# A two-layer graph attention kernel: where and when head 0's softmax sums of layer 1 are added, and when its accumulators are copied

## The chip, the cores and the metric

The kernel runs on one core of a Trainium2 chip. Its time is the device time of one execution in microseconds (us): a median over several runs, and one further execution that the hardware profiler recorded.

A core has five engines that run their own instruction queues in order and wait for each other through semaphores: TensorE (PE in the profile, with its weight loads as PEld), VectorE (DVE), ScalarE (ACT), GpSimd (POOL) and SyncE (SP). Transfers run on 16 DMA engines; SP and POOL issue most of them.

## What is computed

The reference, cut to what matters here. `x` is 4096 x 512, `adj` is 4096 x 4096 of zeros and ones; all is float32.

```python
# layer 0: h = relu(layernorm(x)); masked attention of 4096 x 4096 scores
x = x + L0_gnn_ref(h, adj, ...)
# layer 1: h = relu(layernorm(x)); 8 heads of 64 columns
data1 = (h @ W.T + b).reshape(4096, 8, 64)
src = jnp.einsum('nhd,xhd->nh', data1, src_proj)
trg = jnp.einsum('nhd,xhd->nh', data1, trg_proj)
e = src.T[:, :, None] + trg.T[:, None, :]      # heads x n x m
e = jnp.where(e >= 0, e, 0.01 * e)             # leaky ReLU
e = e + adj[None, :, :]
scores = jax.nn.softmax(e, axis=-1)
out = jnp.einsum('hnm,hmd->hnd', scores, data1.transpose(1, 0, 2))
x = x + out.transpose(1, 0, 2).reshape(4096, 512)
```

The change touches layer 1 alone.

## The kernel before

Layer 1 works on blocks of 1024 rows n (`WL`) and groups of four heads (`HG`): 4 x 2 = 8 groups `i`, one after the other. Inside a group it walks over 32 tiles `m` of 128 neighbours. A tile's scores lie as 128 neighbours (partitions) x 1024 rows. There are thus 256 steps, and in each step a hand-written list (`stages`) calls one function for each engine's work, some of them for tiles that lie ahead: `load` 4 tiles ahead, `exps` 1, `weigh` 1, `factors` 2, `logs` 4, `scale` 2, `gather` 0. The schedule is manual: each engine's queue has exactly the order of these calls.

What one tile costs each engine:

- SP: `load` fetches one tile of the transposed adjacency (`e`, L1066, four buffers).
- ACT: `exps` makes `ex = exp(adj)` into PSUM (L1088, one buffer). `last_exps` makes a scaled copy of it in SBUF for head 3 (`e`, L1098). `relus` makes `rl` for head 0 (L1121). In every fourth tile (`BY_LOG`: m = 3, 7, ... 31) head 0 is made on another way: `logs` (L1104) makes a ReLU, `add_logs` (L1110) adds the adjacency to it on POOL in two halves, and an exponential (L1118) gives head 0's weights directly.
- DVE: `weigh` makes the unnormalised weights `pr` of the four heads, one instruction each, in the order 3, 0, 1, 2 (`ORDER`). Heads 1 and 2 take `ex` from PSUM (L1139, `pr<-z,g_m,ex`); head 3 takes its factor from SBUF (L1139, `pr<-z,g_m,e`); head 0 takes `ex` too (L1136), and is not there in the `BY_LOG` tiles. `pr` of heads 1 to 3 has two buffers each, of head 0 three.
- PE: `gather` multiplies the weights with the values into four PSUM accumulators `pv` (L1174: 16 matmuls of 32 columns of the array, each of which shows as two instructions) and adds the softmax denominators into `dn` (L1179). Four matmuls run side by side on four groups of 32 columns.
- POOL: it adds head 3's weights into an accumulator (`acc3`, L1150; L1148 for the first two tiles). Behind it, it issues an accumulating transfer that adds head 0's weights of the tile into one of two accumulators in SBUF (L1157; plain copies for m = 0 and 1, L1155). It runs `add_logs` too: the second half for tile m + 1 ahead of the sum (and, by a wait written by hand, behind head 3's product), the first half for tile m + 2 behind it.

Head 0's sums of a tile are made either by that transfer (24 tiles, `BY_DMA`) or by PE as two extra matmuls with ones (the tiles 6, 10, 14, 18, 22, 26, 29 and 31). In the last tile PE adds the accumulators into `dn` as well.

At a group's end `gather` copies the four accumulators `pv` to SBUF on ACT (`os`, L1207). In the next group's steps `finish` then copies the denominators (`od`, L1213), inverts them, transposes the outputs two tiles at a time (`pt`, L1233), scales them (L1260), adds `x1` to them with an accumulating transfer that POOL issues (L1265), and sends them out on SP (L1263). It advances by one piece in the steps `PARTS`. After the last group `finish_last` does the same work at once.

Of the kernel before, what the change touches and what calls it, by code (L numbers as in the profile page):

```python
# [8 lines left out]
FP = mybir.dt.float32  # L9
# [6 lines left out]
P = 128  # L16
# [12 lines left out]
def kernel(  # L29
# [941 lines left out]
    nlg_m = l1.tile([P, H // HG, NT], FP, name="nlg_m")  # L971
    d0_m = l1.tile([P, H // 2, NT, 2], FP, name="d0_m")
    d0_0 = l1.tile([P, H // 2, P // 4], FP, name="d0_0")
    zo = l1.tile([P, 3], FP, name="zo")

# [19 lines left out]

    PARTS = (0, 1, 2, 4, 5, 6, 8, 9, 10, 12, 13, 14, 16, 17, 18)  # L1000
    BY_LOG = (3, 7, 11, 15, 19, 23, 27, 31)
    BY_DMA = [m for m in range(NT) if m not in (6, 10, 14, 18, 22, 26, 29, 31)]
    after = mybir.DependencyInfo(mybir.DependencyClass.Sync, mybir.DependencyReason.DATA)

    with tc.tile_pool(name="p", bufs=2) as prp, tc.tile_pool(name="s0", bufs=1) as s0, tc.tile_pool(
# [14 lines left out]
        us = {}  # L1020
        zs_, ra, ex, e3, rl, pr, acc, pv, late = {}, {}, {}, {}, {}, {}, {}, {}, {}
        ORDER = (3, 0, 1, 2)
        for t, val in ((d0_0, 0.0), (d0_m, 0.0), (zo[:, 0:2], 0.0), (zo[:, 2:3], 1.0)):
            nc.gpsimd.memset(t, val)

        def tables():
# [27 lines left out]
        row = ident.rearrange("p (r s) -> p s r", s=Q)  # L1054
        nc.vector.tensor_copy(pick, row[:, 0:2, :])
        nc.vector.tensor_tensor(pick[:, 1, 0:HV], pick[:, 1, 0:HV], row[:, 2, HV:2 * HV], ALU.add)

        def zload(i, k):
            b, g = groups[i]
# [38 lines left out]
            nc.scalar.activation(x_, ra[i, m], AF.Exp, bias=ld_m[:, h // HG, m:m + 1])  # L1098
            e3[i, m] = x_

        def logs(i, m):
            if m in BY_LOG:
                r = rlp.tile([P, WL], FP, name="lg", bufs=1)
                nc.scalar.activation(r, us[i], AF.Relu, bias=nlg_m[:, groups[i][1], m:m + 1], scale=-(1.0 - SLOPE))  # L1104
                rl[i, m] = r

        def add_logs(i, m, half, behind=None):
            if m in BY_LOG:
# [5 lines left out]
        def relus(i, m):  # L1114
            h = groups[i][1] * HG
            if m in BY_LOG:
                pr[i, m, 0] = pr0p.tile([P, WL], FP, name="pr0")
                nc.scalar.activation(pr[i, m, 0], rl.pop((i, m)), AF.Exp, bias=t_m[:, h, m:m + 1])  # L1118
                return
            r = rlp.tile([P, WL], FP, name="rl")  # L1120
            nc.scalar.activation(r, zs_[i, 0], AF.Relu, bias=ngd_m[:, h // HG, m:m + 1], scale=d_m[:, h, m:m + 1])  # L1121
            rl[i, m] = r

        def weigh(i, m, order=ORDER):
            h = groups[i][1] * HG
            x_ = ex.pop((i, m))
            for k in order:
                if (i, m, k) in pr:
                    continue
                w = (prp if k else pr0p).tile([P, WL], FP, name=f"pr{k}")  # L1130
                if k == 0 and (i, m) == (0, 0):
                    r = rlp.tile([P, WL], FP, name="rl")
                    nc.vector.tensor_scalar(r, zs_[0, 0], g_m[:, 0, 0:1], d_m[:, 0, 0:1], ALU.max, ALU.mult)
                    nc.vector.tensor_tensor(w, r, x_, ALU.mult)
                elif k == 0:
                    nc.vector.scalar_tensor_tensor(w, rl.pop((i, m)), ngd_m[:, h // HG, m:m + 1], x_,  # L1136
                                                   op0=ALU.subtract, op1=ALU.mult)
                else:
                    p_ = nc.vector.scalar_tensor_tensor(w, zs_[i, k], g_m[:, h + k, m:m + 1],  # L1139
                                                        e3.pop((i, m)) if k == 3 else x_,  # L1140
                                                        op0=ALU.max, op1=ALU.mult)
                    if k == 3:
                        add_logs(i, m + 1, 1, p_)
                pr[i, m, k] = w
            w = pr[i, m, 3]
            if m == 1:
                acc[i, 3] = acp.tile([P, WL], FP, name="acc3", bufs=1)
                nc.gpsimd.tensor_tensor(acc[i, 3], pr[i, 0, 3], w, ALU.add)  # L1148
            elif m > 1:
                nc.gpsimd.tensor_tensor(acc[i, 3], acc[i, 3], w, ALU.add)  # L1150
            add_logs(i, m + 2, 0)
            if m == 1:
                for n in range(2):
                    acc[i, 0, n] = acp.tile([P, WL], FP, name=f"acc0{n}", bufs=1)
                    nc.gpsimd.dma_start(acc[i, 0, n], pr[i, n, 0])  # L1155
            elif m > 1 and m in BY_DMA:
                nc.gpsimd.dma_start(acc[i, 0, (len(BY_DMA) + BY_DMA.index(m)) % 2], pr[i, m, 0], accum_op=ALU.add)  # L1157

        def gather(i, m):
            b, g = groups[i]  # L1160
# [2 lines left out]
                pv[i] = ([[p_v.tile([P, BL], FP, name=f"pv{c}{q}") for q in range(HV)] for c in range(2)],  # L1163
                         p_v.tile([P, BL], FP, name="dn"))
            v, dn = pv[i]
            by_pe = [u for u in range(NT) if u not in BY_DMA]
            side = sum(u < m for u in by_pe) % 2

            def values(c):
                for q in range(HV):  # L1170
                    for r in (side, 1 - side):
                        k = ((3, 0), (1, 2))[c][r]
                        for c0 in range(0, D, Q):
                            nc.tensor.matmul(v[c][q][r * D + c0:r * D + c0 + Q, :],  # L1174
                                             va[:, m, g * HG + k, c0:c0 + Q],
                                             pr[i, m, k][:, q * BL:(q + 1) * BL], start=(m == 0), stop=last)

            def den(r, w, src, q, **fl):
                nc.tensor.matmul(dn[r * Q:r * Q + w.shape[1], :], w, src[:, q * BL:(q + 1) * BL], **fl)  # L1179

            values(0 if (i, m) != (0, 0) else 1)
            if last:
                for r, a in enumerate((acc[i, 0, 0], acc[i, 3])):
                    for q in range(HV):
                        den(r * HV + q, zo[:, 1:3], a, q, start=False, stop=False)
                if m in by_pe:
                    for q in range(HV):
                        den(side * HV + q, zo[:, 1 - side:3], pr[i, m, 0], q, start=False, stop=False)
            values(1 if (i, m) != (0, 0) else 0)
            for r in (side, 1 - side):  # L1190
                for q in range(HV):
                    hk = g * 2 + r
                    den(r * HV + q, d0_m[:, hk, m, :] if m else d0_0[:, hk, :], pr[i, m, r + 1], q,
                        start=(m == 0), stop=(last and r == 1))
            if m in by_pe and not last:
                for q in range(HV):
                    den(side * HV + q, zo[:, 1 - side:3], pr[i, m, 0], q, start=False, stop=False)
            if last:
                for q in range(HV):
                    den(q, zo[:, 1:3], acc[i, 0, 1], q, start=False, stop=True)  # L1200
            for k in range(HG):
                pr.pop((i, m - 1, k), None)
            if last:
                os_ = [[osp.tile([P, BL], FP, name=f"os{c}{q}") for q in range(HV)] for c in range(2)]
                for c in range(2):
                    for q in range(HV):
                        nc.scalar.copy(os_[c][q], v[c][q])  # L1207
                late[i] = os_, dn

        def denominators(i):  # L1210
            os_, dn = late.pop(i)
            od = osp.tile([P, BL], FP, name="od")
            nc.scalar.copy(od, dn)  # L1213
            yield os_
            pd = p_t.tile([P, JT, 2, 4], FP, name="pt")
            for j in range(JT):
                nc.tensor.matmul(pd[:, j, :, :].rearrange("p e r -> p (e r)"), od[:, j * P:(j + 1) * P],  # L1217
                                 pick.rearrange("p e r -> p (e r)"), start=True, stop=True)
            yield
            rd = s0.tile([P, JT, 2, 4], FP, name="rd", bufs=2)  # L1220
            nc.vector.reciprocal(rd, pd)
            yield rd

# [18 lines left out]
        def finish(i):  # L1242
# [5 lines left out]
            next(dens)  # L1248
            yield
            rd = next(dens)  # L1250
            old = None
            for t in range(0, WT, 2):
                pt = p_t.tile([P, 2, HG, D], FP, name="pt")
                for j in range(2):
                    turn(os_, t + j, pt[:, j, :, :])
                yield
                o = iop.tile([P, 2, HG, D], FP, name="o")
                for j in range(2):
                    for r, k in enumerate(ORDER):
                        nc.scalar.activation(o[:, j, k, :], pt[:, j, r, :], AF.Copy, scale=share(rd, t + j, r))  # L1260
                    if j == 0:
                        if t:
                            nc.sync.dma_start(part(out, i, t - 2, 2), old)  # L1263
                        yield
                nc.gpsimd.dma_start(o, part(x1, i, t, 2), accum_op=ALU.add)  # L1265
                old = o
                yield
            nc.sync.dma_start(part(out, i, WT - 2, 2), old)
            yield

        def finish_last(i):

            ys = [ep.tile([P, WT // 2, HG, D], FP, name="e") for _ in range(2)]
            for n in range(2):
                nc.sync.dma_start(ys[n], part(x1, i, n * WT // 2, WT // 2))
            yield
            dens = denominators(i)
            os_ = next(dens)
            pts = []
# [65 lines left out]
        weigh(0, 0, (3, 1, 2, 0))  # L1345
        nc.vector.scalar_tensor_tensor(ngd_m, g_m[:, 0::HG, :], -1.0, d_m[:, 0::HG, :], op0=ALU.mult, op1=ALU.mult)  # L1346
        factors(0, 1)
        logs(0, 3)
        scale(0, 1)

        stages = ((load, 4), (exps, 1), (weigh, 1), (factors, 2), (logs, 4), (scale, 2), (gather, 0))
        for s in range(len(steps)):
            for f, ahead in stages:
                if s + ahead < len(steps):
# [47 lines left out]
```

## Time and profile before

| | us |
|---|---|
| median of 3 runs | 2816.33 (2816.02 to 2816.9) |
| the profiled execution: its time | 2822.91 |
| its span, first to last instruction | 2821.0 |
| layer 1's matmuls, first to last start | 1617.8 to 2809.0 |

The granted clock of TensorE was 0.993 over the span. From 2300 to 2450 us, a stretch of 150 us inside layer 1, PE is busy for 148.81 us, DVE for 147.47, ACT for 121.88 and POOL for 119.05, and the DMA engines for 0.92 of the time. The issue of a transfer is listed on POOL with a duration of its own. Tiles have no names in the profile; a tile can be told by its instructions, since only a `BY_LOG` tile has no L1136 on DVE.

In the views below, a row of the timeline is: start, duration (both us), engine, line, operation, output<-inputs, shape, count, and in brackets how long the engine had been idle before it and what ended that. A row of the waits is: who waited, for whom, total us, times, longest.

### The profile page before, as it was taken

What the parts mean: (1) busy time and instruction counts of PE and PEld (TensorE: products, weight loads), DVE (VectorE), ACT (ScalarE), POOL (GpSimd) and SP (SyncE); (2) the same over time, 40 slices, a digit from 0 to 9 for tenths busy, and PEclk for the clock granted to TensorE, in tenths of its full rate; (3) what the DMA queues carried; (4) which work ended last, traced back from release to release, by engine and by line L of the source; (5) the groups of instructions that cost most, each with busy time, mean ns of one, the idle gap of its engine ahead of it and who ended that gap; (6) DMA issues with size and microseconds to landing.
All of it is one profiled execution on the core that took longest, in us unless ns stands there. A gap on an engine that the chain in (4) does not pass through costs nothing. (4 is left out here: it accounts for less than half of the span.)

```text
span 2821.0 us, 46842 instructions
## 1 busy us (share of the span) xinstructions
PE 2758.7 (98%) x16843; PEld 1491.2 (53%) x16843; DVE 2506.5 (89%) x3424; ACT 1474.5 (52%) x2218; POOL 1396.5 (50%) x1178
## 2 busy tenths in 40 slices
PE   7999999998999999999999899999999999999998
PEld 4885444444888888888885323323222222232222
DVE  7877798898888888888886799999999999999998
ACT  2212232332124333433432188988788878888786
POOL 5323344444011010011106687887878787878786
PEclk9999999999999999999999999999999999999999
DMA  5636898887999999999977389989999998989896
GB/s 174 176 102 253 273 337 300 306 291 232 194 215 204 185 275 191 222 267 204 230 191 195 96 202 235 248 211 246 219 244 223 240 222 236 229 239 219 213 223 168
DMA packets 535992, 629.86 MB, mean 223 GB/s; under 512 B 292152, under 2 KB 346456, under 8 KB 535760
## 3 DMA queue, kind: packets, MB, share of 16 engines
q1 hardware_dynamic: 461920, 415.87, 49.5%
q0 software_dynamic: 71824, 207.07, 33.8%
q10 hardware_dynamic: 2016, 3.93, 0.4%
q8 instruction: 132, 2.16, 0.3%
q14 instruction: 100, 0.82, 0.1%
HBM read 404.23 MB, written 107.15 MB: 181 GB/s over the span
## 5 line engine op out<-in xcount | busy, mean ns | idle before, releaser
L1174 PE MATMUL pv<-pr,sup 128*32 128x512 f32 x8192 | 988.9, 594 | 8.6 <-POOL d L1344 6.2
L1150 POOL TENSOR_TENSOR acc<-acc,pr 128x1024 f32<-128x1024 f32 x240 | 577.0, 2404 | 149.3 <-DVE pr L1139 147.4
L1139 DVE SCALAR_TENSOR_TENSOR pr<-z,g_m,ex 128x1024 f32<-128x1024 f32 x512 | 630.4, 1271 | 4.1 <-ACT ex L1088 2.8
L1174 PEld LDWEIGHTS pv<-pr,sup 128*32 128x32 f32 x8192 | 283.8, 110 | 607.8 <-issue 544.9
L525 PE MATMUL pe<-he_t,he_t 128*128 128x512 f32 x896 | 389.3, 595 | 0.0
L692 ACT ACTIVATE d<-d 128x1024 f32<-128x1024 f32 x126 | 133.1, 1056 | 442.6 <-DVE d L684 230.7
L1139 DVE SCALAR_TENSOR_TENSOR pr<-z,g_m,e 128x1024 f32<-128x1024 f32 x256 | 345.3, 1349 | 3.3 <-PE pv L1174 2.8
L1088 ACT ACTIVATE ex<-e 128x1024 f32<-128x1024 f32 x256 | 263.2, 1028 | 143.2 <-DVE pr L1139 142.4
L1179 PE MATMUL dn<-pr,d_m 128*2 128x512 f32 x1984 | 319.1, 592 | 0.0
L1098 ACT ACTIVATE e<-e,ld_m 128x1024 f32<-128x1024 f32 x256 | 290.9, 1136 | 0.0
L525 PEld LDWEIGHTS pe<-he_t,he_t 128*128 128x128 f32 x896 | 170.3, 191 | 210.1 <-issue 194.8
L731 PE MATMUL po<-he_t,at 128*128 128x256 f32 x1024 | 263.8, 380 | 6.0 <-ACT he_t L742 6.0
L731 PE MATMUL po<-sup,u 128*128 128x256 f32 x1024 | 263.3, 379 | 0.0
L1136 DVE SCALAR_TENSOR_TENSOR pr<-rl,ngd_m,ex 128x1024 f32<-128x1024 f32 x191 | 242.6, 1270 | 10.3 <-ACT ex L1088 10.3
L731 PE MATMUL po<-sup,at 128*128 128x256 f32 x1024 | 243.4, 381 | 3.5 <-DVE at L702 2.3
L1121 ACT ACTIVATE rl<-z,ngd_m,d_m 128x1024 f32<-128x1024 f32 x191 | 234.8, 1229 | 1.3 <-DVE ngd_m L1346 1.3
L818 POOL DMA_DIRECT2D he_t<-he_t x56 | 48.7, 948 | 351.6 <-ACT he_t L734 299.1
L702 DVE TENSOR_TENSOR at<-d,a 128x1024 f32<-128x1024 f32 x126 | 154.1, 1223 | 71.7 <-PE po L731 34.4
L731 PEld LDWEIGHTS po<-he_t,at 128*128 128x128 f32 x1024 | 195.0, 191 | 32.9 <-issue 6.4
L731 PEld LDWEIGHTS po<-sup,at 128*128 128x128 f32 x1024 | 194.8, 191 | 32.3 <-DVE at L702 4.5
L731 PEld LDWEIGHTS po<-sup,u 128*128 128x128 f32 x1024 | 193.9, 190 | 26.0
L530 POOL DMA_DIRECT2D er_d<-mk x136 | 74.5, 548 | 239.3 <-DVE rm L527 227.2
(268 smaller groups left out, 3823.4 us busy)
## 6 DMA issues: line engine op xcount, KB each, us to landing
e<-in_adj_t_dram SPq DMA_DIRECT2D x256, 512.0 KB, 5.9
acc<-pr POOLq DMA_DIRECT2D x192, 512.0 KB, 5.9
a<-in_adj_t_dram SPq DMA_DIRECT2D x126, 512.0 KB, 5.5
ac<-in_adj_t_dram SPq DMA_DIRECT2D x124, 256.0 KB, 5.1
ar<-in_adj_dram SPq DMA_DIRECT2D x120, 256.0 KB, 4.9
ec_d<-mc POOLq DMA_DIRECT2D x120, 256.0 KB, 5.1
er_d<-mk POOLq DMA_DIRECT2D x112, 256.0 KB, 4.8
et<-er_d SPq DMA_DIRECT2D x448, 64.0 KB, 3.9
```

The costliest lines, as they stand in the source:

```text
L525: nc.tensor.matmul(pe[:, :w], he_t[i][:, k, (t % TB) * P:(t % TB + 1) * P], he_t[j][:, k, BL - w:], start=(k == 0), stop=(k == KC - 1))
L692: nc.scalar.activation(d, d, AF.Exp)
L702: nc.vector.tensor_tensor(w, d, aj.pop((n, q)), ALU.mult)
L731: nc.tensor.matmul(acc[:, j, :], A[:, j * P:(j + 1) * P], B, start=(first_ and j == 0), stop=last, skip_group_check=True)
L1088: nc.scalar.activation(x_, ra.pop((i, m)), AF.Exp)
L1098: nc.scalar.activation(x_, ra[i, m], AF.Exp, bias=ld_m[:, h // HG, m:m + 1])
L1121: nc.scalar.activation(r, zs_[i, 0], AF.Relu, bias=ngd_m[:, h // HG, m:m + 1], scale=d_m[:, h, m:m + 1])
L1136: nc.vector.scalar_tensor_tensor(w, rl.pop((i, m)), ngd_m[:, h // HG, m:m + 1], x_, op0=ALU.subtract, op1=ALU.mult)
L1139: p_ = nc.vector.scalar_tensor_tensor(w, zs_[i, k], g_m[:, h + k, m:m + 1], e3.pop((i, m)) if k == 3 else x_, op0=ALU.max, op1=ALU.mult)
L1150: nc.gpsimd.tensor_tensor(acc[i, 3], acc[i, 3], w, ALU.add)
L1174: nc.tensor.matmul(v[c][q][r * D + c0:r * D + c0 + Q, :], va[:, m, g * HG + k, c0:c0 + Q], pr[i, m, k][:, q * BL:(q + 1) * BL], start=(m = ...
L1179: nc.tensor.matmul(dn[r * Q:r * Q + w.shape[1], :], w, src[:, q * BL:(q + 1) * BL], **fl)
```

## The change

1. Head 0's sums. `BY_HALF` = (4, 8, ... 28) takes the place of the tiles that PE summed alone: of such a tile, columns 0 to 511 are summed by PE with one extra matmul (before: two), and columns 512 to 1023 by POOL into a third accumulator `acc02`, behind head 3's sum. Tile 31 stays with PE. The transfers stay 24 a group; they now also cover tiles such as 6, 10 and 29, and no longer 4, 8, ... 28. PE's four column groups are taken in an order that rotates by one with each `BY_HALF` tile.
2. The transfers' place in POOL's queue. `sums(i, m - 1)` issues tile m - 1's transfer in `weigh(m)`, behind `add_logs` of tile m + 1 and ahead of head 3's sum of tile m. The two first copies are issued one by one in the same way. The output's accumulating transfer is put on a list and issued at the same place, in a tile with m % 4 == 1; the transfer of the output to DRAM follows one piece later than before (`PARTS` gets a piece more, 22).
3. ACT's order at a group's end. Only the first accumulator is copied in `gather`. The other three and the denominators are copied in the next step (`rest`), behind that step's `exps`. The ReLU of tile 3 (`early_logs`) is made one step earlier.
4. The first tile of all now takes heads 3 and 0 ahead of 1 and 2 on PE, as all others do; `pick` gets three more small adds.

```diff
-    PARTS = (0, 1, 2, 4, 5, 6, 8, 9, 10, 12, 13, 14, 16, 17, 18)
+    PARTS = (0, 1, 2, 4, 5, 6, 8, 9, 10, 12, 13, 14, 16, 17, 18, 22)
     BY_LOG = (3, 7, 11, 15, 19, 23, 27, 31)
-    BY_DMA = [m for m in range(NT) if m not in (6, 10, 14, 18, 22, 26, 29, 31)]
+    BY_HALF = (4, 8, 12, 16, 20, 24, 28)
+    BY_DMA = [m for m in range(NT - 1) if m not in BY_HALF]
...
+        for c in range(1, 4):
+            nc.vector.tensor_tensor(pick[:, 1, 0:1], pick[:, 1, 0:1], row[:, 3, c:c + 1], ALU.add)
...
-        def logs(i, m):
-            if m in BY_LOG:
+        def logs(i, m, early=False):
+            if m in BY_LOG and early == (m == BY_LOG[0]):
...
+        due = []
+
+        def sums(i, m):
+            if m < 2:
+                acc[i, 0, m] = acp.tile([P, WL], FP, name=f"acc0{m}", bufs=1)
+                nc.gpsimd.dma_start(acc[i, 0, m], pr[i, m, 0])
+            elif m in BY_DMA:
+                nc.gpsimd.dma_start(acc[i, 0, (len(BY_DMA) + BY_DMA.index(m)) % 2], pr[i, m, 0], accum_op=ALU.add)
...
             w = pr[i, m, 3]
+            if m % 4 == 1 and due:
+                due.pop()()
+            if m:
+                sums(i, m - 1)
             if m == 1:
                 acc[i, 3] = acp.tile([P, WL], FP, name="acc3", bufs=1)
                 nc.gpsimd.tensor_tensor(acc[i, 3], pr[i, 0, 3], w, ALU.add)
             elif m > 1:
                 nc.gpsimd.tensor_tensor(acc[i, 3], acc[i, 3], w, ALU.add)
             add_logs(i, m + 2, 0)
-            if m == 1:
-                for n in range(2):
-                    acc[i, 0, n] = acp.tile([P, WL], FP, name=f"acc0{n}", bufs=1)
-                    nc.gpsimd.dma_start(acc[i, 0, n], pr[i, n, 0])
-            elif m > 1 and m in BY_DMA:
-                nc.gpsimd.dma_start(acc[i, 0, (len(BY_DMA) + BY_DMA.index(m)) % 2], pr[i, m, 0], accum_op=ALU.add)
+            if m == BY_HALF[0]:
+                acc[i, 0, 2] = acp.tile([P, BL], FP, name="acc02", bufs=1)
+                nc.gpsimd.tensor_copy(acc[i, 0, 2], pr[i, m, 0][:, BL:])
+            elif m in BY_HALF:
+                nc.gpsimd.tensor_tensor(acc[i, 0, 2], acc[i, 0, 2], pr[i, m, 0][:, BL:], ALU.add)
...
-            values(0 if (i, m) != (0, 0) else 1)
+            values(0)
             if last:
-                for r, a in enumerate((acc[i, 0, 0], acc[i, 3])):
-                    for q in range(HV):
-                        den(r * HV + q, zo[:, 1:3], a, q, start=False, stop=False)
-                if m in by_pe:
-                    for q in range(HV):
-                        den(side * HV + q, zo[:, 1 - side:3], pr[i, m, 0], q, start=False, stop=False)
+                for q in range(HV):
+                    ones(q, 1, halves(acc[i, 0, 0])[q])
+                for q in range(HV):
+                    ones(HV + q, 1, halves(acc[i, 3])[q])
+                ones(1, 1, acc[i, 0, 2])
+                for q in range(HV):
+                    ones(HV + q, 2, halves(pr[i, m, 0])[q])
+            values(1)
...
-            if m in by_pe and not last:
-                for q in range(HV):
-                    den(side * HV + q, zo[:, 1 - side:3], pr[i, m, 0], q, start=False, stop=False)
+            if m in BY_HALF:
+                ones(n, 3 if n else 1, halves(pr[i, m, 0])[0])
...
-                for c in range(2):
-                    for q in range(HV):
-                        nc.scalar.copy(os_[c][q], v[c][q])
-                late[i] = os_, dn
+                nc.scalar.copy(os_[0][0], v[0][0])
+                late[i] = os_, v, dn
+
+        def rest(i, m):
+            if i and m == 0:
+                copy_rest(i - 1)
+
+        def copy_rest(i):
+            os_, v, dn = late[i]
+            for c, q in ((0, 1), (1, 0), (1, 1)):
+                nc.scalar.copy(os_[c][q], v[c][q])
+            od = iop.tile([P, BL], FP, name="o")
+            nc.scalar.copy(od, dn)
+            late[i] = os_, od
...
+                if t > 2:
+                    nc.sync.dma_start(part(out, i, t - 4, 2), old.pop(0))
                 yield
...
-                        if t:
-                            nc.sync.dma_start(part(out, i, t - 2, 2), old)
...
-                nc.gpsimd.dma_start(o, part(x1, i, t, 2), accum_op=ALU.add)
-                old = o
+                old.append(o)
+                due.append(lambda o=o, t=t: nc.gpsimd.dma_start(o, part(x1, i, t, 2), accum_op=ALU.add))
...
-        logs(0, 3)
+        early_logs(0, 3)
...
-        stages = ((load, 4), (exps, 1), (weigh, 1), (factors, 2), (logs, 4), (scale, 2), (gather, 0))
+        stages = ((load, 4), (exps, 1), (rest, 0), (weigh, 1), (factors, 2), (logs, 4), (early_logs, 5), (scale, 2), (gather, 0))
```

More of the change, by code (lines that the diff above doesn't have):

```diff
@@ L973 @@
     d0_0 = l1.tile([P, H // 2, P // 4], FP, name="d0_0")
-    zo = l1.tile([P, 3], FP, name="zo")
+    zo = l1.tile([P, 4], FP, name="zo")
     HV = WL // BL
@@ L1022 @@
         ORDER = (3, 0, 1, 2)
-        for t, val in ((d0_0, 0.0), (d0_m, 0.0), (zo[:, 0:2], 0.0), (zo[:, 2:3], 1.0)):
+        for t, val in ((d0_0, 0.0), (d0_m, 0.0), (zo[:, 0:3], 0.0), (zo[:, 3:4], 1.0)):
             nc.gpsimd.memset(t, val)
@@ L1105, in logs, with early_logs @@
                 rl[i, m] = r
+        def early_logs(i, m):
+            logs(i, m, True)
         def add_logs(i, m, half, behind=None):
@@ L1165, in gather @@
             v, dn = pv[i]
-            by_pe = [u for u in range(NT) if u not in BY_DMA]
-            side = sum(u < m for u in by_pe) % 2
+            n = sum(u < m for u in BY_HALF) % 4
+            cols = [(n + c) % 4 for c in range(4)]
             def values(c):
                 for q in range(HV):
-                    for r in (side, 1 - side):
+                    for col in cols:
+                        r, c0 = col // 2, col % 2 * Q
                         k = ((3, 0), (1, 2))[c][r]
[L1173 to L1176, printed above, removed]
@@ L1178, in den @@
-            def den(r, w, src, q, **fl):
-                nc.tensor.matmul(dn[r * Q:r * Q + w.shape[1], :], w, src[:, q * BL:(q + 1) * BL], **fl)
-            values(0 if (i, m) != (0, 0) else 1)
-            if last:
-                for r, a in enumerate((acc[i, 0, 0], acc[i, 3])):
-                    for q in range(HV):
-                        den(r * HV + q, zo[:, 1:3], a, q, start=False, stop=False)
-                if m in by_pe:
-                    for q in range(HV):
-                        den(side * HV + q, zo[:, 1 - side:3], pr[i, m, 0], q, start=False, stop=False)
@@ L1189, in gather @@
-            values(1 if (i, m) != (0, 0) else 0)
-            for r in (side, 1 - side):
-                for q in range(HV):
-                    hk = g * 2 + r
-                    den(r * HV + q, d0_m[:, hk, m, :] if m else d0_0[:, hk, :], pr[i, m, r + 1], q,
-                        start=(m == 0), stop=(last and r == 1))
-            if m in by_pe and not last:
-                for q in range(HV):
-                    den(side * HV + q, zo[:, 1 - side:3], pr[i, m, 0], q, start=False, stop=False)
+                        nc.tensor.matmul(v[c][q][col * Q:(col + 1) * Q, :],
+                                         va[:, m, g * HG + k, c0:c0 + Q],
+                                         pr[i, m, k][:, q * BL:(q + 1) * BL], start=(m == 0), stop=last)
@@ L1198, in gather, with den, ones, halves @@
+            def den(col, w, src, **fl):
+                nc.tensor.matmul(dn[col * Q:col * Q + w.shape[1], :], w, src, **fl)
+            def ones(col, row, src, stop=False):
+                den(col, zo[:, 3 - row:4], src, start=False, stop=stop)
+            def halves(src):
+                return [src[:, q * BL:(q + 1) * BL] for q in range(HV)]
+            values(0)
             if last:
                 for q in range(HV):
-                    den(q, zo[:, 1:3], acc[i, 0, 1], q, start=False, stop=True)
+                    ones(q, 1, halves(acc[i, 0, 0])[q])
[4 more added lines that the diff above has]
+                    ones(HV + q, 2, halves(pr[i, m, 0])[q])
@@ new lines, in gather @@
+            values(1)
+            for col in cols:
+                r, q = divmod(col, HV)
+                hk = g * 2 + r
+                den(col, d0_m[:, hk, m, :] if m else d0_0[:, hk, :], halves(pr[i, m, r + 1])[q],
+                    start=(m == 0), stop=(last and r == 1))
+            if m in BY_HALF:
+                ones(n, 3 if n else 1, halves(pr[i, m, 0])[0])
+            if last:
+                for q in range(HV):
+                    ones(q, 1, halves(acc[i, 0, 1])[q], True)
@@ L1204, in gather @@
                 os_ = [[osp.tile([P, BL], FP, name=f"os{c}{q}") for q in range(HV)] for c in range(2)]
-                for c in range(2):
-                    for q in range(HV):
-                        nc.scalar.copy(os_[c][q], v[c][q])
-                late[i] = os_, dn
+                nc.scalar.copy(os_[0][0], v[0][0])
[10 more added lines that the diff above has]
+            late[i] = os_, od
         def denominators(i):
-            os_, dn = late.pop(i)
-            od = osp.tile([P, BL], FP, name="od")
-            nc.scalar.copy(od, dn)
+            os_, od = late.pop(i)
             yield os_
@@ L1219, in denominators @@
             yield
-            rd = s0.tile([P, JT, 2, 4], FP, name="rd", bufs=2)
+            rd = sp.tile([P, JT, 2, 4], FP, name="rd", bufs=2)
             nc.vector.reciprocal(rd, pd)
@@ L1250, in finish @@
             rd = next(dens)
-            old = None
+            old = []
             for t in range(0, WT, 2):
@@ L1261, in finish @@
                     if j == 0:
-                        if t:
-                            nc.sync.dma_start(part(out, i, t - 2, 2), old)
                         yield
-                nc.gpsimd.dma_start(o, part(x1, i, t, 2), accum_op=ALU.add)
-                old = o
+                old.append(o)
+                due.append(lambda o=o, t=t: nc.gpsimd.dma_start(o, part(x1, i, t, 2), accum_op=ALU.add))
                 yield
-            nc.sync.dma_start(part(out, i, WT - 2, 2), old)
+            nc.sync.dma_start(part(out, i, WT - 4, 2), old.pop(0))
+            yield
+            nc.sync.dma_start(part(out, i, WT - 2, 2), old.pop(0))
             yield
@@ L1276, in finish_last @@
             yield
+            copy_rest(i)
             dens = denominators(i)
```

## The prediction

> **What bounds the kernel now.** I read the page's totals first, then the waits of layer 1, then the timelines of DVE, POOL and PE, one tile after the other. The page, its busy times, costliest groups and transfers:
>
> ```profile
> PE 2758.7 (98%) x16843; PEld 1491.2 (53%) x16843; DVE 2506.5 (89%) x3424; ACT 1474.5 (52%) x2218; POOL 1396.5 (50%) x1178
> ...
> L1150 POOL TENSOR_TENSOR acc<-acc,pr 128x1024 f32<-128x1024 f32 x240 | 577.0, 2404 | 149.3 <-DVE pr L1139 147.4
> ...
> acc<-pr POOLq DMA_DIRECT2D x192, 512.0 KB, 5.9
> ```
>
> In layer 1, PE and DVE are both all but full (148.81 and 147.47 of 150 us), so neither total says which one leads. The waits between 1640 and 2800 us:
>
> ```profile
> POOL acc L1150 <- DVE pr L1139: 147.0, 144, 2.1
> ...
> ACT pr L1118 <- DMA acc<-pr: 26.2, 14, 3.0
> ...
> PEld dn L1179 <- ACT od L1213: 11.7, 7, 2.1
> ...
> DVE pr L1136 <- ACT ex L1088: 8.2, 7, 1.2
> ```
>
> DVE hardly waits for anyone by this view. The timeline of 1868 to 1906 us shows a wait that it hides, inside an instruction's duration (POOL and DVE rows):
>
> ```profile
> 1871.22 0.84 POOL L1157 DMA_DIRECT2D acc<-pr  x1
> ...
> 1871.84 1.54 POOL L1110 TENSOR_TENSOR lg<-lg,e 128x512 f32<-128x512 f32 x1
> 1873.09 2.64 POOL L1150 TENSOR_TENSOR acc<-acc,pr 128x1024 f32<-128x1024 f32 x1
> ...
> 1873.61 3.20 DVE L1139 SCALAR_TENSOR_TENSOR pr<-z,g_m,e 128x1024 f32<-128x1024 f32 x1
> ...
> 1887.73 1.27 POOL L1110 TENSOR_TENSOR lg<-lg,e 128x512 f32<-128x512 f32 x1
> 1888.71 1.38 DVE L1139 SCALAR_TENSOR_TENSOR pr<-z,g_m,e 128x1024 f32<-128x1024 f32 x1
> ...
> 1888.95 0.84 POOL L1157 DMA_DIRECT2D acc<-pr  x1
> ...
> 1890.18 1.28 POOL L1110 TENSOR_TENSOR lg<-lg,e 128x512 f32<-128x512 f32 x1 [0.39 <-DVE pr L1139]
> ...
> 1891.43 2.37 POOL L1150 TENSOR_TENSOR acc<-acc,pr 128x1024 f32<-128x1024 f32 x1
> ...
> 1893.59 1.31 DVE L1139 SCALAR_TENSOR_TENSOR pr<-z,g_m,e 128x1024 f32<-128x1024 f32 x1
> ...
> 1895.04 2.42 POOL L1150 TENSOR_TENSOR acc<-acc,pr 128x1024 f32<-128x1024 f32 x1 [1.23 <-DVE pr L1139]
> 1897.20 1.33 DVE L1139 SCALAR_TENSOR_TENSOR pr<-z,g_m,e 128x1024 f32<-128x1024 f32 x1
> ...
> 1898.69 2.39 POOL L1150 TENSOR_TENSOR acc<-acc,pr 128x1024 f32<-128x1024 f32 x1 [0.47 <-DVE pr L1139]
> ```
>
> Head 3's product (`pr<-z,g_m,e`) takes 1.27 us when it is let through at once. It took 3.20 where a sum on POOL was running: 3.20 - 1.27 puts its real start at 1875.54, and the sum ended at 1873.09 + 2.64 = 1875.73. At 1888.71 it took 1.38, so it began at 1888.82, and POOL's add ended at 1889.00. In both it begins 0.18 to 0.19 before the end of POOL's add; the other products, which take `ex` from PSUM, keep their 1.27 whatever POOL does. So head 3's product and an add on POOL exclude each other. A transfer's issue does not take part (1888.95 lies inside the product), but it holds up POOL's next add: the 1.54 of the add behind the issue at 1871.22 is 0.22 until the issue's end plus 1.28 of its own, and on the add's heels the sum slid into the product.
>
> **The pace of both engines.** Four tiles are a cycle; I call its tiles A, B, C, D (m % 4 = 1, 2, 3, 0; C has no head 0 on DVE). The rows above are the cycle m = 25 to 28. DVE's own cycle is 18.09 us (head 0's products of two D tiles begin at 1898.46 and 1916.55). Eight cycles are 144.7, plus 1.2 idle at a group's start for `ex` (1.17 at 1922.56): 145.9 a group. PE's tile is 4.29 (ten steps of 0.43, four matmuls abreast). Its groups begin at 1770.33, 1920.48, 2069.16, 2217.50, 2365.64, 2514.39 and 2662.09: 148.6 on average. From the third group on PE leads, and DVE has some 2.5 us a group to spare, 0.3 a cycle.
>
> **Part 2, the transfers' place.** On POOL, tile A's transfer was issued in the gap between the two halves of `add_logs` (1888.95, while the second half waited for head 3's product). It now stands behind the second half. Worked on the rows above: that half ends at 1891.46; then 0.84 of issue; the sum of B begins some 0.80 later than 1891.43 and ends at 1894.6 in place of 1893.80. Head 3's product of C, due at 1893.59, gets through at 1894.43: 0.80 late, all of it on DVE's path, since heads 1 and 2 and the next exponential follow it in order. B's transfer is new there (tile 26 had none); its issue lies beside C's product, which lasts 1.27. C's sum then ends at 1898.26, and D's product, due at 1898.00, at 1898.08. C's transfer was behind C's sum before and still is.
>
> Two waits come nearer. The accumulators alternate, so C's transfer waits on POOL for A's to land, 6.75 us after A's issue; queued behind it are D's sum, the half sum and the next `add_logs`, and head 3's product waits for those. The page's median is 5.9 us, and single ones took up to 10.9. With 0.5 us of slack ahead of D's sum I charge nothing; at 9 us it would be 1.7 a cycle. Head 0's product of D reuses A's buffer 7.8 us after A's issue: nothing at 5.9 either. The wait of ACT's exponential for a transfer (26.2 us) goes, since the buffer it reuses now belongs to a D tile; DVE's 18.09 never contained it, so no gain is booked beyond reaching that pace.
>
> The output's accumulating transfer (L1265, 1.23 of issue) now lies beside A's product, 1.27, ahead of A's sum: nothing, and 1.2 if POOL came late there. Its send on SP follows at least a tile after; behind it on SP is the load of a tile four ahead, which needs a buffer that frees later. Nothing.
>
> **Part 1, head 0's sums.** POOL gets half a sum in each D, no row of its own; nearest is the 128x512 add, 1.28 (bounds: 0 if wholly beside DVE's other products, 1.28 if wholly ahead of A's product). By place: D's sum ends at 1901.9, the half at 1903.14; A's product, due at 1902.03 + 0.82, gets through at 1902.96. That is 0.1 late. So a cycle grows by 0.8 + 0.1 = 0.9, to 19.0.
>
> [...]
>
> PE loses six column matmuls a group, 22 to 16. Counted per column group it gains nothing: before, the tiles 6, 10 and 14 each left half a step empty before the full-width transposes of `finish`; now one extra matmul on one column does the same (0.86 each). Behind tile 14 each column had four extra; now column 1 still has four (tile 24 and three at the end).
>
> **Part 3, ACT at a group's end.** PE's wait for `od` (11.7 in the loads' row, about 7 us of real delay) goes, since `od` is ready about 1.5 us earlier: worth 1.0 a group where PE leads, nothing where DVE does. DVE's 1.17 for `ex` goes too. Against it, the earlier ReLU puts four ACT instructions (starts 4.26 apart) into the C tile of 3.6 us: `ex` of tile 0 is 0.65 late, DVE 0.45; and three copies and `od` (4 x 0.49) make `ex` of tile 2 late, DVE 0.2. Net -0.5. If the cover for these copies goes, PE waits up to 0.4 for the second accumulator.
>
> **Part 4.** Three small adds ahead of the first product: 3 x 0.1 = +0.3. PE's first tile begins about 4 us later, covered by DVE, which leads in the first group.
>
> **The sum.** A group has seven full cycles, 7 x 0.9 = 6.3; the first copy transfer in tile 2 adds 0.5 in the same way; part 3 takes 0.5. DVE's group: 145.9 + 6.3 = 152.2, against PE's 147.6: DVE leads everywhere. In DVE's times, from head 3's first product at 1615.10 to its last at 2800.48, 1185.4 before: the first group took 150.05 and gets 6.8, 156.9; six groups at 152.2 are 913.2; the last, short of one 3.6 us tile, 148.6. Together 1218.7, or +33.3. PE ends about 1 us closer behind DVE; +0.3 from part 4. Net +32: the span goes from 2821.0 to 2853. That execution took 2822.91, 6.6 above the median, which I carry as it is: 2816.3 + 32 = 2848.
>
> **Rivals.**
> Deeper (0.12): A, B and C transfers, 3.2 us apart where two were 3.6 apart, queue up and take 8 to 9 us. DMA at 0.92 speaks for it; 7.8 us of buffer against a 5.9 median, and the long gap before A, against it. Price: about 0.8 in four cycles of seven groups, +22: 2870.
> Faster (0.08): an issue behind an add leaves POOL free for the next add, so the sum does not slide, and only 0.1 a cycle comes. DVE's 18.2 then stays below PE's pace, PE leads, and `od` gives 1.0 in seven groups, the missing stalls of the second group 2: 2816.3 - 8 = 2808. The 1.54 row speaks against it. It decides once the slide is under 0.3 a cycle.
> No net change (0.05): part of the slide is made good by stalls that vanish, at a cycle of 18.5, where DVE just meets PE: 2816.
>
> **How the numbers follow.** The forecast has 0.75, 2832 to 2864 by itself (the cycle between 18.75 and 19.2, seven cycles in eight groups, and a few us of transfer waits). With part of the deeper case the range is 2828 to 2868. A measurement tells 0.2% (5.6 us) from no change. Slower 0.87, the same 0.05, faster 0.08.
>
> **What would show it.** After the change, head 3's product of C should take about 2.1 us in place of 1.31, each time ending 1.1 after a sum on POOL; head 0's products of D tiles should begin 19.0 apart; PE should wait for DVE in every group; DVE's 1.17 for `ex` and PE's wait for `od` should be gone. A product of C at 1.3 us would make the prediction wrong, and so would C's transfer on POOL waiting for microseconds.

## The result, and the profile after

| | before | after |
|---|---|---|
| median, us | 2816.61 (2816.02 to 2817.21, 4 runs) | 2857.76 (2854.89 to 2859.91, 4 runs) |
| profiled execution: time, span | 2822.91, 2821.0 | 2857.73, 2855.9 |
| head 3's products on DVE, first to last start | 1615.10 to 2800.48: 1185.4 | 1611.10 to 2835.63: 1224.5 |
| from the last of them to the span's end | 20.5 | 20.3 |

The changed kernel is slower: the ratio of the runs is 1.0142, with a 95% interval of 1.0130 to 1.0154 (the two medians alone give 1.0146). The profiled executions are only 34.8 us apart, because that of before lay 6.3 us above its median, while that of after lies on its own. Some 4 of these 6.3 us lie ahead of layer 1, whose first product begins at 1615.10 in the one and at 1611.10 in the other. Layer 1 itself grew by 39 us.

The page of the changed kernel, its busy times, two of its costliest groups and a row of its transfers:

```profile
PE 2784.0 (97%) x16747; PEld 1518.8 (53%) x16747; DVE 2560.7 (90%) x3427; ACT 1477.5 (52%) x2218; POOL 1467.6 (51%) x1234
...
L1169 POOL TENSOR_TENSOR acc<-acc,pr 128x1024 f32<-128x1024 f32 x240 | 593.4, 2472 | 87.4 <-DVE pr L1154 84.2
...
L1154 DVE SCALAR_TENSOR_TENSOR pr<-z,g_m,e 128x1024 f32<-128x1024 f32 x256 | 401.5, 1568 | 0.0
...
acc<-pr POOLq DMA_DIRECT2D x192, 512.0 KB, 7.6
```

DVE is 54 us busier, with three instructions more. That is no work: head 3's product, now L1154, takes 1568 ns on average, where it took 1349 (345.3 us in all) before. The 256 of them thus took 401.5 - 345.3 = 56.2 us longer, which are waits that the profile counts as busy time. DVE's other long groups kept their 1270 ns. POOL's sum of head 3 waits less for DVE (84.2 us, 147.4 before), since it is now the late one of the two. The transfers take 7.6 us to land instead of 5.9; from the second group on it is 6.0 for those of A tiles, and 8.4 and 8.3 for those of B and C (medians).

The waits of the changed kernel between 1640 and 2830 us (who waited, for whom, total us, times, longest):

```profile
POOL acc L1169 <- DVE pr L1154: 83.7, 134, 1.8
...
PEld pv L1192 <- DVE pr L1154: 71.8, 112, 1.4
PEld pv L1192 <- DVE pr L1151: 36.4, 78, 1.6
...
PEld dn L1197 <- DMA acc<-pr: 8.6, 9, 2.1
...
POOL acc L1137 <- DMA acc<-pr: 3.2, 5, 0.9
```

PE's loads wait 108 us for DVE's products, 36 before (25.9 and 9.9). In each of the last six groups it is 14.6 to 17.5 us, where it was 3.6 to 6.6: there DVE leads. Only 3.2 us are POOL's waits for a transfer. ACT's wait for a transfer, PE's for `od` and DVE's for `ex` have no row of any size left. One cycle shows where the 56 us sit (POOL and DVE rows of the timeline; DVE's heads 1 and 2 are left out):

```profile
2499.72 1.26 POOL L1175 TENSOR_TENSOR acc<-acc,pr 128x512 f32<-128x512 f32 x1
...
2500.70 1.37 DVE L1154 SCALAR_TENSOR_TENSOR pr<-z,g_m,e 128x1024 f32<-128x1024 f32 x1
...
2507.01 1.28 POOL L1116 TENSOR_TENSOR lg<-lg,e 128x512 f32<-128x512 f32 x1 [1.17 <-DVE pr L1154]
...
2508.23 0.85 POOL L1137 DMA_DIRECT2D acc<-pr  x1
...
2508.84 2.66 POOL L1169 TENSOR_TENSOR acc<-acc,pr 128x1024 f32<-128x1024 f32 x1
2510.42 2.17 DVE L1154 SCALAR_TENSOR_TENSOR pr<-z,g_m,e 128x1024 f32<-128x1024 f32 x1
...
2511.17 1.15 POOL L1137 DMA_DIRECT2D acc<-pr  x1
```

The second half of `add_logs` (2507.01) ends at 2508.29. Then comes tile A's transfer at its new place, 0.85 us of POOL's queue, and only behind it the sum of B, which ends at 2508.84 + 2.66 = 2511.50. Head 3's product of C was due at 2510.42, and lasts 2.17: at 1.27 of its own it really began at 2510.42 + 2.17 - 1.27 = 2511.32, again 0.18 us before the end of POOL's sum. C's product waits like this in all 49 full cycles of the second to the eighth group, by 0.93 us in the median (0.05 before). At 1.27 each the 256 products would be 325.1 us, so they lose 401.5 - 325.1 = 76.4 now and lost 20.2 before; the C tiles alone make up 57 of the 76. The half sum (2499.72) makes A's product 1.37, 0.1 late.

### The profile page after: what moved, and what is told of

It reads as the page before. It is cut to its first block, busy times and chain, and to the rows that moved or that the text cites. A ratio compares the mean times of both kernels' runs of the same rounds, so it can differ in the third digit from the quotient of the medians.

```text
span 2855.9 us, 46714 instructions
## 1 busy us (share of the span) xinstructions
PE 2784.0 (97%) x16747; PEld 1518.8 (53%) x16747; DVE 2560.7 (90%) x3427; ACT 1477.5 (52%) x2218; POOL 1467.6 (51%) x1234
## 4 chain that ended last, share of the span: by engine, by line
PE 55%; DVE 24%; issue 9%; DMA 5%; ACT 3%; POOL 3%; SPq 1%; DVEq 0%; POOLq 0%; ACTq 0%
PE po L731 26%; DVE pr L1154 17%; PE pe L525 11%; PE bank L267 6%; PE pv L1192 5%; PE po L865 4%; DVE pr L1151 4%; DMA acc<-pr 3%; ACT e L1101 2%; PE dn L1197 2%; POOL acc L1169 1%; DVE mk L514 1%; DMA a<-in_adj_t_dram 1%; DMA xt<-in_x_dram 1%; PE po L751 0%
## 5 line engine op out<-in xcount | busy, mean ns | idle before, releaser
L1192 PE MATMUL pv<-pr,sup 128*32 128x512 f32 x8192 | 1059.0, 595 | 26.3 <-DVE pr L1154 18.5
L1192 PEld LDWEIGHTS pv<-pr,sup 128*32 128x32 f32 x8192 | 310.2, 110 | 629.9 <-issue 462.6
L1169 POOL TENSOR_TENSOR acc<-acc,pr 128x1024 f32<-128x1024 f32 x240 | 593.4, 2472 | 87.4 <-DVE pr L1154 84.2
L1154 DVE SCALAR_TENSOR_TENSOR pr<-z,g_m,ex 128x1024 f32<-128x1024 f32 x512 | 630.0, 1269 | 0.0
L1154 DVE SCALAR_TENSOR_TENSOR pr<-z,g_m,e 128x1024 f32<-128x1024 f32 x256 | 401.5, 1568 | 0.0
L1197 PE MATMUL dn<-pr,d_m 128*2 128x512 f32 x1984 | 363.1, 592 | 0.0
L1151 DVE SCALAR_TENSOR_TENSOR pr<-rl,ngd_m,ex 128x1024 f32<-128x1024 f32 x191 | 242.5, 1270 | 4.5 <-ACT ex L1091 2.1
L1116 POOL TENSOR_TENSOR lg<-lg,e 128x512 f32<-128x512 f32 x128 | 165.0, 1289 | 76.1 <-DVE pr L1154 76.1
```

The costliest lines, as they stand in the source:

```text
L1116: add = nc.gpsimd.tensor_tensor(rl[i, m][:, cs], rl[i, m][:, cs], ra[i, m][:, cs], ALU.add)
L1192: nc.tensor.matmul(v[c][q][col * Q:(col + 1) * Q, :], va[:, m, g * HG + k, c0:c0 + Q], pr[i, m, k][:, q * BL:(q + 1) * BL], start=(m == 0) ...
L1197: nc.tensor.matmul(dn[col * Q:col * Q + w.shape[1], :], w, src, **fl)
```

## The experiments

The kernels of each of the first two sets ran on one chip beside the kernel before; the last two ran as a third set. Medians of the kernel before were 2818.53, 2818.17 and 2817.42. The last column is the mean duration of head 3's product in the profile. Where groups are given, PE's run from one group's first matmul to the next group's, VectorE's from head 3's first product to the next group's.

| kernel | median, us | ratio to before (95%) | product, ns |
|---|---|---|---|
| A's transfer back in the gap | 2815.30 | 0.9987 (0.9978 to 0.9996) | 1349 |
| without the half sums | 2849.37 | 1.0108 (1.0093 to 1.0123) | 1536 |
| before, A's transfer late | 2847.14 | 1.0100 (1.0085 to 1.0116) | 1503 |
| without B's sums | 2820.06 | 1.0008 (0.9998 to 1.0017) | 1354 |
| before, with ACT's order | 2815.44 | 0.9990 (0.9982 to 0.9999) | 1349 |
| the first one again | 2815.43 | 0.9992 (0.9983 to 1.0001) | 1348 |
| tile 28 by transfer | 2816.23 | 0.9993 (0.9984 to 1.0002) | 1364 |
| tiles 4 and 28 by transfer | 2810.96 | 0.9974 (0.9964 to 0.9984) | 1351 |
| B's sums as memsets | 2829.82 | 1.0039 (1.0025 to 1.0053) | 1393 |
| B's sums as copies | 2845.89 | 1.0102 (1.0087 to 1.0117) | 1504 |

**A's transfer back in the gap.** The changed kernel, with one transfer of four put back between the two halves of `add_logs`:

```diff
-            if m:
+            if m and m % 4 != 2:
                 sums(i, m - 1)
...
             add_logs(i, m + 2, 0)
+            if m % 4 == 1:
+                sums(i, m)
```

> The changed kernel with one thing put back: the transfer of an A tile (m % 4 = 1) is issued in the gap between the two halves of add_logs, as before the change; everything else stays. Theory 'slide' (the issue behind the second half pushes head 3's sum of tile B into head 3's product of tile C): that product falls from 2.17 to about 1.31 us, the cycle of four tiles from 19.07 to about 18.2, DVE no longer leads, PE does with 147.6 a group, and the time is 2806 to 2818. Rival 'half sum' (the added sum on POOL is the cost): cycle stays near 19, time 2850 to 2858. Rival 'transfers' (transfers now take 7.6 us to land in place of 5.9, and their landing holds DVE or POOL): only part comes back, 2830 to 2845.

It takes 2815.3 us: the whole loss is gone, and all other parts of the change together are worth a few us. Its timeline over the same part of a cycle:

```profile
2493.88 0.87 POOL L1137 DMA_DIRECT2D acc<-pr  x1
...
2495.12 1.28 POOL L1116 TENSOR_TENSOR lg<-lg,e 128x512 f32<-128x512 f32 x1 [0.38 <-DVE pr L1154]
...
2496.38 2.39 POOL L1169 TENSOR_TENSOR acc<-acc,pr 128x1024 f32<-128x1024 f32 x1
...
2498.53 1.32 DVE L1154 SCALAR_TENSOR_TENSOR pr<-z,g_m,e 128x1024 f32<-128x1024 f32 x1
```

The issue (2493.88) is done by 2494.75, before the second half may start at 2495.12 anyway: it costs nothing there. The sum ends at 2498.77, 0.24 us after the product is due, and the product loses only 0.05. PE leads again, at 147.3 us a group.

**Without the half sums.** The changed kernel with the half sums left out:

```diff
-            if m == BY_HALF[0]:
-                acc[i, 0, 2] = acp.tile([P, BL], FP, name="acc02", bufs=1)
-                nc.gpsimd.tensor_copy(acc[i, 0, 2], pr[i, m, 0][:, BL:])
-            elif m in BY_HALF:
-                nc.gpsimd.tensor_tensor(acc[i, 0, 2], acc[i, 0, 2], pr[i, m, 0][:, BL:], ALU.add)
...
-                ones(1, 1, acc[i, 0, 2])
```

> The changed kernel without the half sums on POOL: head 0's sums of columns 512 to 1023 in the seven tiles 4, 8, ... 28 are left out, and with them the accumulator that took them; all else stays. 'Slide': only the 0.1 a cycle goes that head 3's product of tile A waits for, and a little where a late half sum met it, 6 to 10 us in all: 2846 to 2853; C's product keeps 2.17. 'Half sum': 2814 to 2822. 'Transfers': 2855 to 2858.

2849.4 us, as the slide theory expects. The wait of A's product is gone, C's stays at 0.93 us, and VectorE's groups take 151.7 in place of 152.8. So the half sums cost some 8 to 10 us of the 41 (8.4 by the medians, which are of different sets, and 9.6 by the ratios). A's products, which lose 8.3 us in all in the changed kernel and 0.5 here, account for most of it, 0.14 a tile.

**Before, with A's transfer late.** The kernel before, with this one move alone (for tiles 5 to 25):

```diff
+        def issue(i, m):
+            nc.gpsimd.dma_start(acc[i, 0, (len(BY_DMA) + BY_DMA.index(m)) % 2], pr[i, m, 0], accum_op=ALU.add)
...
             w = pr[i, m, 3]
+            if m % 4 == 2 and m > 2 and m - 1 in BY_DMA:
+                issue(i, m - 1)
...
-            elif m > 1 and m in BY_DMA:
-                nc.gpsimd.dma_start(acc[i, 0, (len(BY_DMA) + BY_DMA.index(m)) % 2], pr[i, m, 0], accum_op=ALU.add)
+            elif m > 1 and m in BY_DMA and m % 4 != 1:
+                issue(i, m)
```

> The kernel before with one part of the change alone: the transfer of an A tile (5, 9, ... 25) is issued in the next step, behind the second half of add_logs and ahead of head 3's sum of tile B. 'Slide': C's product rises from 1.31 to about 2.17 in six cycles of a group, the group from 148.6 to about 151.2, the time to 2834 to 2848. 'Half sum': no change, 2813 to 2820. 'Transfers': the transfers of A and C come closer, 6.7 us, C to D stays; 2817 to 2830, with C's product at 1.31.

This is the opposite test: the kernel before gets the one thing, and loses 28.6 us. The same rows of its timeline:

```profile
1891.12 1.29 POOL L1110 TENSOR_TENSOR lg<-lg,e 128x512 f32<-128x512 f32 x1 [1.16 <-DVE pr L1142]
...
1892.35 0.86 POOL L1125 DMA_DIRECT2D acc<-pr  x1
1892.96 2.67 POOL L1155 TENSOR_TENSOR acc<-acc,pr 128x1024 f32<-128x1024 f32 x1
1894.55 2.18 DVE L1142 SCALAR_TENSOR_TENSOR pr<-z,g_m,e 128x1024 f32<-128x1024 f32 x1
```

The signature is that of the changed kernel (2.18 against 2.17). Transfers land in 5.7 us here (5.9 before); slower landings thus aren't needed for the loss. That it loses less than the 42 us between the changed kernel and the first experiment fits the smaller number of slides (six a group), no half sums, and PE's own slower pace, 148.6, in the kernel before.

**Without B's sums.** The changed kernel with head 3's sum left out in the B tiles, which takes away what slides:

```diff
-            elif m > 1:
+            elif m > 1 and m % 4 != 2:
                 nc.gpsimd.tensor_tensor(acc[i, 3], acc[i, 3], w, ALU.add)
```

> The changed kernel with head 3's sum left out in the B tiles (m % 4 = 2); transfers, their order and the half sums stay. 'Slide' through the exclusion of POOL's add and head 3's product: with no add running there, C's product is let through at once, 1.27 to 1.4 us, the cycle is 18.2 and PE leads: 2806 to 2818. If the issues or the landings of the transfers held DVE themselves, C's product would keep 2.17 and the time 2850 to 2858. 'Half sum': likewise 2850 to 2858.

2820.1 us, 2 above the range. C's product is back at 1.27 us with the transfer at its late place, as these rows show (A's and B's issues stand one behind the other), so the late issue alone does no harm:

```profile
2480.39 1.72 POOL L1137 DMA_DIRECT2D acc<-pr  x2
...
2482.58 1.27 DVE L1154 SCALAR_TENSOR_TENSOR pr<-z,g_m,e 128x1024 f32<-128x1024 f32 x1
```

What keeps it 5 us above the first experiment was not tried by itself. In the trace transfers land in 8.0 us, POOL waits 12.9 us for them, and A's products lose 14.0 us in all, where they lost 5.3 in the first experiment.

**Before, with ACT's order alone** (part 3 of the change), **and the first experiment again** on the same chip:

```diff
-                for c in range(2):
-                    for q in range(HV):
-                        nc.scalar.copy(os_[c][q], v[c][q])
-                late[i] = os_, dn
+                nc.scalar.copy(os_[0][0], v[0][0])
+                late[i] = os_, v, dn
...
-        stages = ((load, 4), (exps, 1), (weigh, 1), (factors, 2), (logs, 4), (scale, 2), (gather, 0))
+        stages = ((load, 4), (exps, 1), (rest, 0), (weigh, 1), (factors, 2), (logs, 4), (early_logs, 5), (scale, 2), (gather, 0))
```

> The kernel before with part 3 of the change alone: ACT's order at a group's end (one accumulator copied in the last tile, the other three and the denominators behind the next step's exponential, the ReLU of tile 3 one step earlier). If PE leads in the kernel before and waits for the denominators' copy, 1.0 us a group goes in seven groups, and PE's groups fall from 148.6 to about 147.6: 2808 to 2813 beside a kernel before at 2816 to 2818. Rival, DVE leads there too: its 1.17 idle is exchanged for 0.65 of new idle, 0 to -4 us: 2813 to 2818.

> The changed kernel with A's transfer back in the gap once more, beside the other two of this set: 2812 to 2816, PE's groups at 147.3. If the half sums on POOL relieve PE of anything, it is below the kernel before with ACT's order alone; counted by column groups it is not, so the two should agree within 2 us.

Both take 2815.4 us. Part 3 was to give about 1.0 us a group; PE's groups went from 148.6 to 148.3 on average, and the time fell by some 3 us (0.3 to 5 by the interval). That misses the expected range and lies in the rival's, whose reason isn't seen either: PE's loads wait for DVE as long as before (36.5 us, 35.8 before). The waits of this kernel between 1640 and 2830 us:

```profile
PEld pv L1177 <- DVE pr L1142: 26.5, 78, 1.3
PEld pv L1177 <- ACT os L1218: 11.5, 13, 1.7
```

PE's wait for `od`, 11.7 us before, is gone, but PE now waits 11.5 us for the accumulators that are copied one step later (1.3 before). So a wait about as long has come at the other accumulators. ACT's wait for a transfer grew too, from 26.2 to 38.9 us. The first experiment, which has six column matmuls less a group as well, is not faster than this by the medians. The prediction's count by columns gave those six no gain; but the two kernels differ in more than that (147.3 against 148.3 us for PE's groups, 151.7 against 150.0 for VectorE's first group), so the medians don't show it by themselves.

**Tile 28, and tiles 4 and 28, by transfer.** The first experiment, with fewer half sums; the first column of the rotation is set apart:

```diff
-    BY_HALF = (4, 8, 12, 16, 20, 24, 28)
+    BY_HALF = (8, 12, 16, 20, 24)
+    FIRST = 0
...
-            n = sum(u < m for u in BY_HALF) % 4
+            n = (FIRST + sum(u < m for u in BY_HALF)) % 4
```

> As the one before, but tile 28's sums go by a transfer (25 a group) and the rotation starts at column 3, so that behind tile 14 each of PE's four column groups has three extra matmuls in place of 3, 4, 3 and 3. If PE leads and its pace goes by the fullest column group, each group loses 0.86: PE's groups at 146.4 and the time 6 to 7 us under the one before. If the count of matmuls in all were what matters (one fewer of 656), nothing is seen: within 2 us of it. Rival, the added transfer lands late for the log tile 31: up to 3 us a group more.

> As the one before, and tile 4's sums go by a transfer too (26 a group), which takes away one of the three steps that PE leaves three quarters empty ahead of its transposes: another 0.86 a group by the count of column groups, PE's at 145.6. DVE's own group is near 145.3 there, so it is the last that PE can give: 4 to 7 us under the one before. Rival: DVE or ACT (log tile 7 reuses tile 4's buffer) leads already: no change or slower by up to 10.

The first of the two (with 4 left in and `FIRST = 3`) missed. From one tile's first matmul to the next, tile 28 fell from 5.13 to 4.29 us as expected, but tile 31 rose from 6.03 to 6.85. The count by the fullest column, which held in the tiles before, does not hold in the last tile; which matmul's place decides there was not settled. The second one takes 2810.96 us, faster than both kernels: its PE groups take 146.6 us, where 145.6 was expected. Tile 6, the one behind tile 4, fell from 5.82 to 4.99 us as the count says; tile 31 stayed at 6.85.

**What keeps the product out.** The changed kernel, with B's sums replaced by two memsets of the accumulator, or by two copies into it (`nc.gpsimd.tensor_copy(acc[i, 3], w)` in place of the memset); head 3's sums of the B tiles are left out in both:

```diff
+            elif m % 4 == 2:
+                for _ in range(2):
+                    nc.gpsimd.memset(acc[i, 3], 0.0)
             elif m > 1:
```

> The changed kernel, but in the B tiles head 3's sum is replaced by two memsets of the same accumulator on GpSimd, which write as many bytes and read nothing; head 3's sums of the B tiles are left out. Two memsets of 128x1024 last 2 x 1.23 = 2.46 us by layer 0's row, as long as the sum (2.47), at the same place in the queue. Theory that it is the sum's reads from SBUF that exclude head 3's product: C's product takes 1.27 to 1.40 beside the second memset, VectorE's groups fall from 152.8 to 147 to 149 us, and the time is 2816 to 2826 us, as in the kernel without those sums (2820). Rival, that a product with two SBUF inputs excludes any long GpSimd instruction: C's product takes 1.9 to 2.2 and the time is 2848 to 2860.

> The same with two copies of head 3's weights into the accumulator in place of the two memsets: one read and one write for each element, instead of two reads and a write once; head 3's sums of the B tiles are left out here too. By the 128x512 copy (0.82 us) a 128x1024 copy lasts some 1.2 to 1.6 us. Theory of the reads: C's product begins about 0.18 us before the second copy's end and takes 1.9 to 2.9 us, and the time is 2846 to 2876. If C's product took 1.27 to 1.40 here too, and the time were 2816 to 2826, the lock would need an instruction with two inputs on GpSimd's side. The rival of the kernel with memsets (any long GpSimd instruction) expects the same here as the theory of the reads: the pair of kernels tells them apart.

A cycle with memsets:

```profile
2491.47 0.85 POOL L1137 DMA_DIRECT2D acc<-pr  x1
...
2492.04 2.27 POOL L1170 MEMSET acc<- 128x1024 f32 x2
2493.66 1.27 DVE L1154 SCALAR_TENSOR_TENSOR pr<-z,g_m,e 128x1024 f32<-128x1024 f32 x1
...
2495.08 2.44 POOL L1172 TENSOR_TENSOR acc<-acc,pr 128x1024 f32<-128x1024 f32 x1
2497.24 1.38 DVE L1154 SCALAR_TENSOR_TENSOR pr<-z,g_m,e 128x1024 f32<-128x1024 f32 x1
```

And with copies:

```profile
2482.02 2.46 POOL L1170 COPY acc<-pr 128x1024 f32<-128x1024 f32 x2
2483.62 1.93 DVE L1154 SCALAR_TENSOR_TENSOR pr<-z,g_m,e 128x1024 f32<-128x1024 f32 x1
```

The memsets run until 2494.31, and C's product takes its 1.27 us beside them; no C product of the 49 lost more than 0.01. The copies run until 2484.48, and the product begins at 2483.62 + 1.93 - 1.27 = 2484.28, 0.20 us before their end. In both, POOL is busy at the due time and writes the same accumulator; only the copies read SBUF. So it is POOL's reading that keeps the product out, and one input is enough. The memset kernel's time is 4 us above what the theory gave it, and its trace shows the next product in the row late: B's transfer is issued behind the memsets, C's sum begins behind that and ends at 2497.52, and D's product (2497.24) takes 1.38. D's products lose 7.9 us in all here, and nothing in the kernel without B's sums. DVE's waits for landing transfers are longer too (4.6 us, 1.7 there). The copy kernel took 0.1 us less than its range.

## Why the prediction was right, and where its sizes were off

- **The mechanism was right.** The prediction had A's issue push B's sum by 0.8 us into C's product, and all of that on DVE's path. The two opposite experiments show it: undone in the changed kernel, the loss goes (2815.3); made alone in the kernel before, 28.6 us come.
- **C's product** was to take about 2.1 us; it takes 2.20 in the median, 0.88 more than before where 0.80 was counted. The cycle is 19.09 us (median) for 19.0, and a group 152.8 for 152.2. Over the seven later groups this is 4 us of what was missed. The issue holds POOL for 0.85, and the sum passes the shift on whole.
- **A's product** was to be 0.1 late; it is (1.27 to 1.37), and goes back without the half sums, which are worth some 8 to 10 us; by the prediction's 0.1 a tile the 56 of them are 5.6. Its upper bound of 1.28 a tile did not come.
- **The first group** was given 6.8 us and took 8.8. There POOL also scales the values (`sup`, L1085), which the prediction left out. Head 3's products of the tiles 3 to 7 come 0.3 to 1.4 late in the trace (before, tiles 4 and 6 alone were, by 0.6). That the scaling is the cause is not shown by an experiment.
- **The end** was to be 1 us shorter. From the last product's start to the end it is 20.5 before and 20.3 after. But this product is a C, and waits too. Its rows before and after:

```profile
2800.48 1.31 DVE L1139 SCALAR_TENSOR_TENSOR pr<-z,g_m,e 128x1024 f32<-128x1024 f32 x1
...
2835.63 2.17 DVE L1154 SCALAR_TENSOR_TENSOR pr<-z,g_m,e 128x1024 f32<-128x1024 f32 x1
```

From its end it is 19.2 before and 18.1 after: the 1 us came, and the last C's own 0.86, which the prediction did not count there, took most of it back. PE's waits for transfers (8.6 us) lie at the ends of the first seven groups and none in this stretch.

- **Part 3** was mis-sized. The waits named, for `od` and `ex`, are gone as foretold, but "worth 1.0 a group where PE leads" is 0.3 in the kernel before: PE waits 11.5 us for the delayed copies there, 1.6 a group, where the prediction named 0.4 at most. In the changed kernel this hardly counts, because DVE leads there. The 0.5 a group that the prediction gave DVE for part 3 was not tried by itself.
- **Transfers.** POOL's waits for a landing were charged nothing and are 3.2 us in the layer. Half of the deeper rival came: B's and C's transfers took 8.4 and 8.3 us. Its price of 22 us did not, since the landing that POOL's next issue waits for is A's, which took 6.0, and C's issue comes 6.9 us behind A's. That of an issue that leaves POOL free fell with the 2.17 us product; that of no net change fell with the cycle of 19.09. (The terms of the faster rival give 9 us, not 8.)
- **Part 4** (0.3 us) was not tried by itself.
- **The sum.** 33.3 us were counted from the first to the last of head 3's products, and 39.15 came: 2.0 in the first group, 3.5 in the next six, 0.3 in the last. The end adds 0.8. The other 3 us of the gap between 2848 and 2857.8 lie outside these terms: the profiled execution of before was 6.3 above its median, and 4.0 of that lay ahead of layer 1.

## What to carry to other kernels

An instruction that another engine's instruction keeps out can show as busy and long, not as idle (C's product here: 2.17 us, for 1.27 of its own): compare one instruction's duration with that of its fastest peers before believing a list of waits. A transfer's issue costs the issuing engine its own time (0.85 us of POOL's here); put it into a gap where that engine waits anyway, not ahead of an instruction that another engine will run into. Taking a wait off one accumulator by delaying the copies of others can move the wait to these (11.7 us at the denominators became 11.5 at the delayed accumulators, in the kernel before with ACT's order), so look at who needs each of them next.

## What the runs showed of the hardware

- One read from SBUF on GpSimd was enough to keep head 3's product on VectorE, which takes two tensors from SBUF, out until 0.20 us before the end of GpSimd's instruction (1.93 us beside copies), while memsets of the same size did not delay it (1.27 us).
- A product that has waited begins 0.16 to 0.20 us before the recorded end of the GpSimd instruction, beside sums of head 3, half sums, adds to `lg` and copies alike (all 156 of the products over 1.29 us in the kernel before, 227 of 228 in the changed kernel; 0.20 beside a copy).
- The same number of accumulating transfers of 512 KB landed in 5.9 us (median) in the kernel before, in 6.6 with the changed kernel's tiles and A's transfer in the gap, in 7.6 with A's, B's and C's issued within 6.9 us (2508.23 to 2515.09 in the cycle above), and in 8.0 without B's sums, where B's follows A's by 0.6 us in place of 2.9 (medians). In the changed kernel A's took 6.0; B's and C's took 8.4 and 8.3.
